# A four-layer graph network on one core: layers 0 and 1 in slots of written order

## The chip, the cores and the metric

The kernel runs on one core of one Trainium2 chip. The metric is device time in microseconds (us): the time of one execution, as a median over runs. A core has five engines that each execute their own stream of instructions: TensorE (PE, matrix products; weight loads are listed apart as PEld), VectorE (DVE), ScalarE (ACT), GpSimd (POOL) and SyncE (SP). They wait for each other through semaphores. Transfers (DMA) are issued by SP, ACT or POOL and run on 16 DMA engines. On-chip memory is SBUF (data) and PSUM (results of PE, in banks of 128 x 512 f32).

## The reference, cut to what matters

`x` is 2708 x 512, `adj` a sparse 2708 x 2708 matrix of non-negative weights whose rows and columns get sparser with their index; all in f32.

```
# layer 0: graph convolution
adj_hat = adj + I;  d = 1/sqrt(rowsum(adj_hat))
x = layernorm(x + (d * adj_hat * d) @ x @ W.T + b)
# layer 1: incidence sum
head = (adj > 0) / max(sqrt(count of positives in the row), EPS)
inc  = adj + head
x = layernorm(x + (inc @ x) / rowsum(inc))
# layer 2: attention over the same neighbours
e  = where(adj != 0, exp(-leaky_relu(s_left + s_right)), 0)
x_a = (e / (rowsum(e) + 1e-5)) @ (x @ W_sa);  x_b = adj @ (x @ W_gcnb) + b_gcnb
x = layernorm(x + sigmoid(attn_a * x_a + attn_b * x_b))   # attn_a, attn_b: gates from adj @ x and x
# layer 3: signs
x = layernorm(x + relu(adj @ (max(sign(x), 0) @ sign(W3).T)))
```

## The kernel before, in words

The 2708 rows are 22 blocks of 128 (the last has 20). Block 0 holds the densest rows and uses all columns. Every other block uses only the columns in which it has a non-zero: up to nine tiles of 128 gathered rows (`ROOM`), many of them for one half of the block's rows only (`HALVES`), plus a few direct tiles (`DIRECT`). Over the blocks these are 107 gathered tiles per layer. Blocks are handled in the order `sequence`: 0, 1, 21, 2, 3, ..., 20.

A first phase (0 to 224 us) loads `adj`, looks for the non-zero columns, gathers the packed weights `packed[b]` and computes `y = x @ W0.T`. It runs inside `in_order()` (L592): instructions traced within it get a dependence on the one before them of the same engine, so that each engine executes them as the program is written. Everything after is ordered by a scheduler, which may put an instruction of a later block before a waiting one of an earlier block on the same engine.

**Layer 0** (224 to 402 us). For each block `b`, POOL gathers rows of `y` by an indirect DMA per tile (`gathered`, L585) into a ring of 10 buffers. PE multiplies each tile with its weights into one PSUM bank (`add_tile`, L1310; two banks of the tag `mm` in turn). DVE adds the bias to the old features (L1401), forms `t` (L1423) and normalises: statistics (L639), aggregate (L641), epsilon (L643), a square root on ACT (L614), a Newton step to the inverse root (L625 to L634), and the scale (L655). SP stores the rows of layer 1's input, `x1_rows`. Between the blocks stand: `count_positive` (L1094, L1096 on DVE, L1098 on PE) and `head_steps` (L1118 to L1150) for layer 1's `head` of each of nine groups of blocks; `attention_columns` (L1335), `attention_rows` and `signs` (L1353, L1354) for later layers; and `grow1` (L1366 to L1370), which adds a finished block's share of block 0's layer 1 sum into the bank `sum1`, two blocks later.

**Layer 1** (402 to 578 us). For each block DVE builds `inc` from the packed weights, up to four tiles at a time (L1564, L1565), POOL gathers rows of `x1_rows` (again L585, 8 buffers), and PE sums (L1310). `finish1` (L1501 on) scales the old features on ACT (L1505), forms `t` on DVE (L1506), normalises with the scale on ACT (L652), multiplies with the row `vr` for the layer 2 score (L1510) and stores `x2_rows` from SP. `grow2` adds one finished block's share of block 0's attention sum, three blocks later: an identity on ACT (L1484), three DVE operations (L1485 to L1487), an exponential (L1488), a copy (L1535), an addition (L1537) and eight products on PE (L1494). ACT holds one set of function tables at a time, so a square root after an exponential reloads them (ACT_TABLE_LOAD), and the other way round. At the start of layer 1 ACT's queue carries the weights of layer 2, the 1 MB `wg` among them.

**Layers 2 and 3** (578 to 1105 us) gather rows of `x2_rows` (L1663) and of `xw_rows`; their code does not change. `open_block` (L1468) opens blocks of layer 2; some of that runs in layer 1.

Of the kernel before, what the change touches and what calls it, by code (L numbers as in the profile page):

```python
# [8 lines left out]
F32 = mybir.dt.float32  # L9
# [5 lines left out]
ALU = mybir.AluOpType  # L15
# [480 lines left out]
def sparse_layers(ctx, tc, x, adj, adj_t, w0_t, b0, w_sa, a_sa, w_gcnb, b_gcnb, wa, ba, wb, bb, w3_t,  # L496
# [140 lines left out]
    def layernorm(dst, t, m: int, name: str, on_pool: bool = False, on_act: bool = False):  # L637
        st = small.tile([P, 6], F32, tag="st", name=f"st_{name}")
        nc.vector.bn_stats(st[:m], t[:m])  # L639
        mv = small.tile([P, 2], F32, tag="mv", name=f"mv_{name}")  # L640
        nc.vector.bn_aggr(mv[:m], st[:m])  # L641
        rs = small.tile([P, 2], F32, tag="rs", name=f"rs_{name}")
        nc.vector.tensor_scalar(mv[:m, 1:2], mv[:m, 1:2], LN_EPS, None, op0=ALU.add)  # L643
        if on_pool:
            nc.gpsimd.tensor_tensor(rs[:m, 0:1], mv[:m, 1:2], neg_half[:m], op=ALU.pow)  # L645
        else:
            rsqrt_of(rs[:m, 0:1], mv[:m, 1:2], m, 1, name)
        if on_act:
            nc.vector.scalar_tensor_tensor(
                rs[:m, 1:2], mv[:m, 0:1], -1.0, rs[:m, 0:1], op0=ALU.mult, op1=ALU.mult  # L650
            )
            return nc.scalar.activation(  # L652
                dst, t[:m], AF.Identity, bias=rs[:m, 1:2], scale=rs[:m, 0:1]
            )
        return nc.vector.tensor_scalar(  # L655
            dst, t[:m], mv[:m, 0:1], rs[:m, 0:1], op0=ALU.subtract, op1=ALU.mult
        )
# [12 lines left out]
    with tc.tile_pool(name="s_pre", bufs=1) as pre:  # L670
# [408 lines left out]
        counts_of = {}  # L1079

        def count_positive(g, pool):

            b0_, G, m = g[0], len(g), rows(g[0])
            hr = ps_s.tile([P, D], F32, tag="find", name=f"hr{b0_}", bufs=2)
            cnt = hr[:, D - GM :]
            counts_of[g] = hr
            at = slice(b0_, b0_ + G)
            nc.vector.tensor_scalar(
                dia_pos[:m, at], dia_own[:m, at], 0.0, None, op0=ALU.is_gt
            )  # L1090
            for k, b in enumerate(g):
                n, nd = tiles(b), len(direct(b))
                valid = small.tile([P, TM], BF16, tag="valid", name=f"valid{b}")
                nc.vector.tensor_scalar(valid[:, : ROOM[b]], index[b], PAD, None, op0=ALU.is_lt)  # L1094
                pos = pool.tile([P, max(ROOM) + 2, P], BF16, tag="pos", name=f"pos{b}", bufs=1)
                nc.vector.tensor_scalar(pos[:, :n, :m], packed[b], 0.0, None, op0=ALU.is_gt)  # L1096
                for i in range(n):
                    nc.tensor.matmul(  # L1098
                        cnt[:m, k : k + 1], pos[:, i, :m],
                        valid[:, i - nd : i - nd + 1] if i >= nd else ones_b,  # L1100
                        start=(i == 0), stop=(i == n - 1),
                    )

        def head_steps(g):
# [8 lines left out]
            def counts():  # L1113
                add_row_sums(g)
                if g == (0,):
                    nc.vector.tensor_tensor(cv, counts0[:, 0:1], counts0[:, 1:2], op=ALU.add)
                else:
                    nc.vector.tensor_tensor(  # L1118
                        cv, counts_of[g][:m, D - GM : D - GM + G], dia_pos[:m, at], op=ALU.add
# [6 lines left out]
            def shares():  # L1126
# [4 lines left out]
                if g == (0,):  # L1131
                    counts_of[g] = ps_s.tile([P, D], F32, tag="find", name="hr0", bufs=2)
                    return
# [5 lines left out]
            def spread():  # L1139
                hr = counts_of[g]  # L1140
# [6 lines left out]
            def keep_heads():  # L1147
                hr = counts_of.pop(g)
# [80 lines left out]


# [86 lines left out]
    with tc.tile_pool(name="s_l0", bufs=10, reuse_waits="tile") as lp:  # L1317
# [22 lines left out]
        def attention_rows():  # L1340
            for s, row in enumerate((vl_row, vr_row)):
                pv = ps_t.tile([P, KC, P], F32, tag="t", name=f"pv{s}")
                for k in range(KC):
                    nc.tensor.transpose(
                        pv[:, k, :], vec[:, s, k : k + 1].to_broadcast([P, P]), ident
                    )
                nc.scalar.copy(row.rearrange("p (k i) -> p k i", i=P), pv)
# [13 lines left out]
        def grow1(j: int):  # L1361
# [14 lines left out]
        between = {  # L1376
            2: [attention_loads], 4: [lambda: attention_columns(0)],
            5: [lambda: attention_columns(1)], 6: [attention_rows],
            8: [lambda: signs(0)], 10: [lambda: signs(1)], 12: [lambda: signs(2)],
            14: [lambda: signs(3)],  # L1380
        }
# [10 lines left out]
        for n, g in enumerate(GROUPS):  # L1392
            steps_ = head_steps(g)
            between.setdefault(2 + 2 * n, []).append(
                several(lambda g=g: count_positive(g, lp), steps_[0])
            )
            between.setdefault(3 + 2 * n, []).append(several(*steps_[1:]))
        for at, b in enumerate(sequence):
            m = rows(b)
            old = place_of_x(b)  # L1400
            nc.vector.tensor_tensor(old[:m, :D], old[:m, :D], b0_row[:m], op=ALU.add)  # L1401
            if b:
# [3 lines left out]
                for i in order_:  # L1406
                    if i >= nd:
                        src[i] = gathered(lp, D, y_rows, b, i - nd)
                    elif direct(b)[i] == b:
                        src[i] = lp.tile([P, D], F32, tag="own", name=f"y_own{b}", bufs=1)  # L1410
# [609 lines left out]
```

## Time and profile before

| | us |
|---|---|
| three runs | 1117.52, 1120.57, 1130.9 (median 1120.57) |
| the profiled execution | 1107.51 |
| its span, first to last instruction | 1105.3 |
| busy in the span: PE, DVE, POOL, ACT | 913.9, 686.0, 522.9, 411.4 |
| layer 0: first gather issued, last gather's end, last store issued | 232.5, 389.1, 401.3 |
| layer 1: the same | 404.2, 559.1, 577.7 |
| layer 2: first and second gather issued | 581.1, 582.4 |
| layer 2: products of block 1's gathered tiles end | 602.2 |

A line of a group names the program's line, the engine, the operation, the tiles it writes and reads and how often it ran; then busy time and the mean of one in ns; then the idle time of that engine just before these instructions and what ended it. A line of waits gives the engine and line that waited, what it waited for, the total in us, how often and the longest. "issue" is time in which nothing shown was waited for. In the chain, each step is followed back from the last instruction to what released it.

### The profile page before, as it was taken

Reading aid. Unit: us, or ns where it says so; the run is one execution under the profiler, and the core shown is the slowest. Engines: PE = TensorE matmul, PEld = TensorE weight load, DVE = VectorE, ACT = ScalarE, POOL = GpSimd, SP = SyncE. Lnnn points to the kernel's source line nnn. Section 1 sums busy time; section 2 is a strip of 40 time slices with the busy share of each in tenths; the row PEclk is TensorE's granted clock in tenths of the full one; section 3 lists DMA queues with packets and bytes.
Section 4 is the critical chain, followed back from the end, with each engine's and each line's share of the span. In section 5 each row is a group of like instructions: output and inputs, shape, how many; then the busy total and the mean of one; then the engine's idle time right before and its main releaser. Section 6 shows DMA issues by size and latency. Waiting matters only on the chain.

```text
span 1105.3 us, 14155 instructions
## 1 busy us (share of the span) xinstructions
PE 913.9 (83%) x4172; PEld 550.5 (50%) x4172; DVE 686.0 (62%) x2812; ACT 411.4 (37%) x918; POOL 522.9 (47%) x539
## 2 busy tenths in 40 slices
PE   3877567768687968888888999999999999889983
PEld 2444334312122312334346577777777777568762
DVE  5766656545565766666774766667667665445665
ACT  3544434300000014556573333333333343254553
POOL 3455555476676637767615143333232232057661
PEclk9888778888889989999999999999999999979996
DMA  9888676276777757767635033332231222289984
GB/s 320 295 275 257 220 241 192 59 218 187 227 212 212 222 164 239 204 204 235 196 116 154 27 110 106 84 104 80 80 106 49 82 79 61 72 257 336 299 248 156
DMA packets 83375, 193.00 MB, mean 175 GB/s; under 512 B 13552, under 2 KB 26712, under 8 KB 83288
## 3 DMA queue, kind: packets, MB, share of 16 engines
q0 software_dynamic: 40048, 111.28, 35.7%
q1 hardware_dynamic: 31548, 65.70, 17.8%
q10 hardware_dynamic: 11692, 15.01, 4.2%
q8 instruction: 35, 0.57, 0.2%
q14 instruction: 52, 0.43, 0.1%
HBM read 156.06 MB, written 25.92 MB: 165 GB/s over the span
## 4 chain that ended last, share of the span: by engine, by line
PE 59%; DVE 11%; issue 8%; another core or an unknown queue 7%; ACT 7%; DMA 6%; POOL 1%; ACTq 0%; SPq 0%; POOLq 0%; DVEq 0%
PE acc L1494 15%; PE l L1310 13%; PE ph L1706 7%; PE l L1889 4%; PE pc L1706 4%; DMA xg<-x_rows,i 4%; PE pg L1706 3%; ACT unused L762 3%; PE l L1928 3%; PE y L1038 2%; PE l L1370 2%; PE px L1756 2%; POOL xg L585 1%; DMA f<-in_x_dram 1%
## 5 line engine op out<-in xcount | busy, mean ns | idle before, releaser
L1663 POOL DMA_INDIRECT xg<-x_rows,i x107 | 105.3, 984 | 158.5 <-PE acc L1494 55.3
L1008 POOL DMA_INDIRECT a<-in_adj_t_dram,row_at x107 | 112.6, 1052 | 116.2 <-DVE s_own L1055 57.2
L585 POOL DMA_INDIRECT xg<-x_rows,i x107 | 106.9, 999 | 63.0 <-issue 24.5
L1494 PE MATMUL acc<-ae,xg 128*128 128x128 f32 (+1 forms) x856 | 125.4, 305 | 6.4 <-ACT ae L1484 2.6
L585 POOL DMA_INDIRECT xg<-y_rows,i x107 | 107.0, 1000 | 49.9 <-issue 24.9
L1494 PEld LDWEIGHTS acc<-ae,xg 128*128 128x128 f32 x856 | 117.0, 191 | 15.8 <-ACT ae L1488 4.1
L1310 PE MATMUL l<-xg,inc 128*64 128x512 f32 (+1 forms) x214 | 91.7, 623 | 17.3 <-DMA xg<-x_rows,i 12.4
L585 POOL DMA_INDIRECT xg<-xw_rows,i x76 | 75.7, 996 | 45.4 <-issue 18.7
L1310 PE MATMUL l<-xg,a 128*64 128x512 f32 (+1 forms) x214 | 92.8, 665 | 2.7 <-issue 1.6
L1038 PE MATMUL y<-s_w,xt 128*128 128x512 f32 (+1 forms) x176 | 93.6, 682 | 0.0
L1706 PE MATMUL ph<-s_wsa,pt 128*128 128x512 f32 (+1 forms) x176 | 79.1, 592 | 0.0
L1494 PE MATMUL acc<-ae,f 128*128 128x256 f32 (+1 forms) x272 | 67.8, 393 | 12.4 <-ACT ae L1535 5.2
L645 POOL TENSOR_TENSOR rs<-mv,s_neg_half 128x1 f32<-128x1 f32 (+1 forms) x22 | 12.6, 571 | 130.4 <-DVE ae L1486 51.4
L1494 PEld LDWEIGHTS acc<-ae,f 128*128 128x128 f32 (+1 forms) x272 | 51.1, 194 | 34.3 <-issue 13.4
L1310 PEld LDWEIGHTS l<-xg,inc 128*64 128x64 f32 (+1 forms) x214 | 24.1, 153 | 74.5 <-issue 43.3
L762 ACT ACTIVATE unused<-arow 128x1408 uint8<-128x1408 f32 (+3 forms) x44 | 58.3, 1325 | 1.5 <-DMA x_rows<-s_zero 0.7
L1484 ACT ACTIVATE ae<-sl,xg 128x64 f32<-128x64 f32 (+1 forms) x107 | 35.9, 362 | 55.7 <-DMA xg<-x_rows,i 28.2
L1038 PEld LDWEIGHTS y<-s_w,xt 128*128 128x128 f32 (+1 forms) x176 | 36.0, 216 | 41.0 <-issue 41.0
L1485 DVE SCALAR_TENSOR_TENSOR ae<-ae 128x128 f32<-128x128 f32 (+4 forms) x95 | 28.2, 297 | 44.2 <-ACT ae L1484 36.1
L1889 PE MATMUL l<-ws,pw 128*128 128x512 f32 (+1 forms) x210 | 52.3, 404 | 2.0 <-DVE pw L1817 2.0
L1928 PE MATMUL l<-xg,p 128*128 128x512 f32 (+1 forms) x152 | 41.6, 418 | 12.2 <-DVE p L1817 11.0
L1706 PE MATMUL pc<-s_wg,pt 128*128 128x258 f32 (+1 forms) x176 | 45.7, 385 | 4.7 <-ACT pt L1693 3.6
(288 smaller groups left out, 1804.8 us busy)
## 6 DMA issues: line engine op xcount, KB each, us to landing
arow<-in_adj_dram SPq DMA_DIRECT2D x21, 704.0 KB
arow<-in_adj_dram SPq DMA_DIRECT2D x21, 650.0 KB
aw<-in_adj_t_dram SPq DMA_DIRECT2D x21, 320.0 KB
x_rows<-f SPq DMA_DIRECT2D x21, 258.0 KB
f<-in_x_dram SPq DMA_DIRECT2D x20, 256.0 KB
y_rows<-yt ACTq DMA_DIRECT2D x20, 256.0 KB
x_rows<-f SPq DMA_DIRECT2D x20, 256.0 KB
out_dram<-f SPq DMA_DIRECT2D x20, 256.0 KB
```

The costliest lines, as they stand in the source:

```text
L585: nc.gpsimd.indirect_dma_start(out=t[:, :dst_w], out_offset=None, in_=src[:, :], in_offset=bass.IndirectOffsetOnAxis(ap=index[b][:, i : i ...
L762: nc.scalar.activation(unused[:m, : ar.shape[1]], ar, AF.Copy, accum_out=row_sums[:m, b, h : h + 1])
L1008: nc.gpsimd.indirect_dma_start(out=packed[b][:, t + len(direct(b)), :], out_offset=None, in_=adj_t, in_offset=bass.IndirectOffsetOnAxis(ap ...
L1038: nc.tensor.matmul(ps[:m], xt[:, k, :m], w0[:, k, :], start=(k == 0), stop=(k == KC - 1))
L1310: nc.tensor.matmul(ps[r0:r1], weights, moving, start=(i == order[0]), stop=all(span(b, j) != (r0, r1) for j in order[order.index(i) + 1 :] ...
L1484: nc.scalar.activation(ev[:, i, :], sl, AF.Identity, bias=score)
L1485: nc.vector.scalar_tensor_tensor(ev, ev, SLOPE, ev, op0=ALU.mult, op1=ALU.max)
L1494: nc.tensor.matmul(acc[:, k, :].rearrange("p (h i) -> p h i", h=2)[:, :, at[0] : at[1]], src[:r, k * P : (k + 1) * P], ae[:r], start=(is_f ...
L1663: nc.gpsimd.indirect_dma_start(out=g, out_offset=None, in_=x2_rows[:, :], in_offset=bass.IndirectOffsetOnAxis(ap=index[b][:, t : t + 1], a ...
L1706: nc.tensor.matmul(ps, pt[:, k, h, :m], w[:, k, :], start=(k == 0), stop=(k == KC - 1))
L1889: nc.tensor.matmul(whole[b], p[:r, h, b * P : (b + 1) * P], g[:r, :], start=(j == 0 and h == 0), stop=(j == NB - 1 and h == 1),)
L1928: nc.tensor.matmul(ps[:m], p[:, h, i * m : (i + 1) * m], src[i0 + i], start=False, stop=(i0 + i == len(src) - 1 and h == 1),)
```

## The change

Layers 0 and 1 are wrapped in `in_order()`, so that each engine executes them as written, and the writing is arranged in slots, one block per slot. A block's sum is started in its slot `at`, and its finish stands two slots later (`LATE = 2`). In layer 0 `grow1` of a block stands four slots after its sum. `layernorm` is split into `layernorm_steps`: between the square root and the Newton step stand the bias addition and `grow1` (layer 0) or `grow2` (layer 1). The sums go through four PSUM banks instead of two, the rings of gather buffers grow from 10 to 13 and from 8 to 11. `count_positive` works one block at a time in slots 1 to 16, the head's spread gets its own PSUM tile, and each `signs(k)` issues its load in its own slot. `inc` is built up to three tiles at a time. In layer 1 `grow2` takes up to three blocks at once; the groups (0,1), (21), (2,3,4), ..., (14,15,16) stand in the loop and (17,18,19) and (20) behind it. The small weight rows of layer 2 are issued from SP instead of ACT, behind the last `x1_rows` store; `wg` and its extra columns move to the start of layer 2, on SP behind the last `x2_rows` store. The sums of `row_sum` are added once, after the first phase.

```diff
+    def layernorm_steps(dst, t, m: int, name: str, on_pool: bool = False, on_act: bool = False):
         st = small.tile([P, 6], F32, tag="st", name=f"st_{name}")
         nc.vector.bn_stats(st[:m], t[:m])
         mv = small.tile([P, 2], F32, tag="mv", name=f"mv_{name}")
         nc.vector.bn_aggr(mv[:m], st[:m])
         rs = small.tile([P, 2], F32, tag="rs", name=f"rs_{name}")
-        nc.vector.tensor_scalar(mv[:m, 1:2], mv[:m, 1:2], LN_EPS, None, op0=ALU.add)
+        v = mv[:m, 1:2]
+        nc.vector.tensor_scalar(v, v, LN_EPS, None, op0=ALU.add)
         if on_pool:
-            nc.gpsimd.tensor_tensor(rs[:m, 0:1], mv[:m, 1:2], neg_half[:m], op=ALU.pow)
+            nc.gpsimd.tensor_tensor(rs[:m, 0:1], v, neg_half[:m], op=ALU.pow)
         else:
-            rsqrt_of(rs[:m, 0:1], mv[:m, 1:2], m, 1, name)
-        if on_act:
-            nc.vector.scalar_tensor_tensor(
-                rs[:m, 1:2], mv[:m, 0:1], -1.0, rs[:m, 0:1], op0=ALU.mult, op1=ALU.mult
-            )
-            return nc.scalar.activation(
-                dst, t[:m], AF.Identity, bias=rs[:m, 1:2], scale=rs[:m, 0:1]
-            )
-        return nc.vector.tensor_scalar(
-            dst, t[:m], mv[:m, 0:1], rs[:m, 0:1], op0=ALU.subtract, op1=ALU.mult
-        )
+            r = small.tile([P, 2, 4], F32, tag="rsqs", name=f"rsqs_{name}")
+            nc.scalar.activation(r[:m, 0, :1], v, AF.Sqrt)
+
+        def rest():
+            if not on_pool:
+                newton(rs[:m, 0:1], v, r[:m, 0, :1], r[:m, 1, :1], 1)
+            if on_act:
+                nc.vector.scalar_tensor_tensor(
+                    rs[:m, 1:2], mv[:m, 0:1], -1.0, rs[:m, 0:1], op0=ALU.mult, op1=ALU.mult
+                )
+                return nc.scalar.activation(
+                    dst, t[:m], AF.Identity, bias=rs[:m, 1:2], scale=rs[:m, 0:1]
+                )
+            return nc.vector.tensor_scalar(
+                dst, t[:m], mv[:m, 0:1], rs[:m, 0:1], op0=ALU.subtract, op1=ALU.mult
+            )
+
+        return rest
...
+        add_row_sums(tuple(range(NB - 1)))
+        add_row_sums((NB - 1,))
...
-    with tc.tile_pool(name="s_l0", bufs=10, reuse_waits="tile") as lp:
+    with tc.tile_pool(name="s_l0", bufs=13, reuse_waits="tile") as lp:
...
+        LATE = 2
+        counted = [(g, k) for g in GROUPS for k in range(len(g))]
+        slot_of = {c: 1 + 16 * n // len(counted) for n, c in enumerate(counted)}
+        for g in GROUPS:
+            last = slot_of[g, len(g) - 1] + LATE
             steps_ = head_steps(g)
-            between.setdefault(2 + 2 * n, []).append(
-                several(lambda g=g: count_positive(g, lp), steps_[0])
-            )
-            between.setdefault(3 + 2 * n, []).append(several(*steps_[1:]))
-        for at, b in enumerate(sequence):
-            m = rows(b)
-            old = place_of_x(b)
-            nc.vector.tensor_tensor(old[:m, :D], old[:m, :D], b0_row[:m], op=ALU.add)
+            put(last + 1, steps_[4])
+            put(last, *steps_[:4])
+        put(20, lambda: attention_spread(0))
+        put(21, lambda: attention_row(0), lambda: attention_spread(1))
+        put(22, lambda: attention_row(1))
+        for c in counted:
+            put(slot_of[c], lambda c=c: count_positive(*c, lp))
+        put(2, attention_loads)
+        put(5, lambda: attention_columns(0))
+        put(7, lambda: attention_columns(1))
+        for k in range(KC):
+            put(9 + 2 * k, lambda k=k: signs(k))
...
-                ps = ps_mm.tile([P, D], F32, tag="mm", name=f"l0_{b}")
+                pool, tag, bufs = SUMS0[at % len(SUMS0)]
+                ps = pool.tile([P, D], F32, tag=tag, name=f"l0_{b}", bufs=bufs)
...
+        def finish0(b: int):
+            m = rows(b)
+            old = place_of_x(b)
             t = work.tile([P, D], F32, tag="t", name=f"t0_{b}")
             nc.vector.scalar_tensor_tensor(
-                t[:m], ps[:m], dinv[:m, b : b + 1], old[:m, :D], op0=ALU.mult, op1=ALU.add
-            )
-            layernorm(old[:m, :D], t, m, f"0_{b}")
-            nc.sync.dma_start(x1_rows[b * P : b * P + m, :], old[:m, :D])
-            for step_ in between.get(at, []):
-                step_()
-        for b in sequence[-2:]:
-            grow1(b)
+                t[:m], sums_of.pop(b)[:m], dinv[:m, b : b + 1], old[:m, :D],
+                op0=ALU.mult, op1=ALU.add,
+            )
+            rest = layernorm_steps(old[:m, :D], t, m, f"0_{b}")
+
+            def store():
+                rest()
+                nc.sync.dma_start(x1_rows[b * P : b * P + m, :], old[:m, :D])
+
+            return store
+
+        SUMS0 = ((ps_mm, "mm", 2), (ps_mm, "sum0", 1), (ps_mm, "mm", 2), (ps_s, "looked", 1))
+        with in_order():
+            for at in range(NB + 2 * LATE):
+                if at < NB:
+                    sum0_of(at, sequence[at])
+                store = None
+                if LATE <= at < NB + LATE:
+                    store = finish0(sequence[at - LATE])
+                if at < NB:
+                    with_bias(sequence[at])
+                if 2 * LATE <= at < NB + LATE:
+                    grow1(sequence[at - 2 * LATE])
+                if store:
+                    store()
+                for step_ in between.get(at, []):
+                    step_()
+                if at >= NB + LATE:
+                    grow1(sequence[at - 2 * LATE])
...
-    wg = wp2.tile([P, KC, D + 2], F32, name="s_wg")
-    nc.scalar.dma_start(wg[:, :, :D], w_gcnb.rearrange("(k p) o -> p k o", p=P))
...
+    with tc.tile_pool(name="s_l1", bufs=11, reuse_waits="tile") as lp:
+        grown2 = []
+
+        def grow2(js):
+
+            r, n, st = rows(js[0]), len(js), state[0]
+            ae = lp.tile([P, G2, 2, P], F32, tag="ae0", name=f"ae0_{js[0]}", bufs=2)
+            av, ev = ae[:r, :n, 0, :], ae[:r, :n, 1, :]
+            a = packed[0][:r, js[0] : js[0] + n, :]
             weights_of(
-                ev[:, None, :], av[:, None, :], st["sl"][:r], a[:, None, :],
-                [f[j][:r, D : D + 1]], f"0_{j}",
+                ev, av, st["sl"][:r], a, [f[j][:r, D : D + 1] for j in js], f"0_{js[0]}"
             )
             nc.scalar.copy(av, a)
-            if n:
-                nc.vector.tensor_tensor(st["esum"][:r], st["esum"][:r], ev, op=ALU.add)
+            if n == 1:
+                nc.vector.tensor_tensor(
+                    st["esum"][:r], st["esum"][:r], ev[:, 0, :], op=ALU.add
+                )
             else:
-                nc.vector.tensor_copy(st["esum"], ev)
-            add_products(0, f[j], ae, r, n == 0, n == NB - 1, (0, P))
-
-        for at, b in enumerate(sequence):
-            m = rows(b)
+                part = st["esum"]
+                if grown2:
+                    part = lp.tile([P, P], F32, tag="part0", name=f"part0_{js[0]}", bufs=1)
+                nc.vector.tensor_reduce(
+                    part[:r, :, None], ev.rearrange("p t i -> p i t"), axis=AX.X, op=ALU.add
+                )
+                if grown2:
+                    nc.vector.tensor_tensor(
+                        st["esum"][:r], st["esum"][:r], part[:r], op=ALU.add
+                    )
+            for i, j in enumerate(js):
+                add_products(
+                    0, f[j], ae[:, i], r, not grown2, len(grown2) == NB - 1, (0, P)
+                )
+                grown2.append(j)
+
+        G2 = 3
+        GROWN2 = [(0, 1), (NB - 1,)] + [
+            tuple(range(j, min(j + G2, NB - 1))) for j in range(2, NB - 1, G2)
+        ]
+        sums_of = {}
+        SUMS1 = (("sum0", 1), ("mm", 2), ("sum1", 1), ("mm", 2))
...
-                for i0, n, (r0, r1) in runs_of(b, 4):
+                for i0, n, (r0, r1) in runs_of(b, 3):
...
+        with in_order():
+            left = list(GROWN2)
+            for at in range(NB + LATE):
+                if at < NB:
+                    sum1_of(at, sequence[at])
+                store = None
+                if at >= LATE:
+                    b = sequence[at - LATE]
+                    store = finish1(b, sums_of.pop(b))
+                if at < NB and left and left[0][-1] in sequence[: max(at - 2 * LATE + 1, 0)]:
+                    grow2(left.pop(0))
+                if store:
+                    store()
+                if at == LATE:
+                    open_block(0, wp2, ps_mm, "mm")
+                    state[0]["acc"] = ps_acc.tile([P, KC, 2 * P], F32, tag="acc", name="acc0")
+            for js in left:
+                grow2(js)
...
+        wg = op.tile([P, KC, D + 2], F32, name="s_wg")
+        nc.sync.dma_start(wg[:, :, :D], w_gcnb.rearrange("(k p) o -> p k o", p=P))
+        pv = ps_s2.tile([P, D], F32, tag="sm", name="pv2")
+        nc.tensor.transpose(pv[:, : 2 * KC], vrows, ident[: 2 * KC, : 2 * KC])
+        nc.vector.tensor_copy(
+            wg[:, :, D:].rearrange("p k t -> p t k"),
+            pv[:, : 2 * KC].rearrange("p (t k) -> p t k", t=2),
```

## The prediction

> **What bounds the kernel now.** I read the page first, then a table of busy time by stage (the stage borders are the first and last instructions of each layer), then the groups and the waits inside layers 0 and 1.
>
> ```profile
> span 1105.3 us, 14155 instructions
> PE 59%; DVE 11%; issue 8%; another core or an unknown queue 7%; ACT 7%; DMA 6%; POOL 1%; ACTq 0%; SPq 0%; POOLq 0%; DVEq 0%
> ```
> ```profile
> 224.00:402.00 178.00, 139.05 (x433) 43.78 (x431) 104.36 (x458) 12.48 (x45) 113.34 (x114) 0.88 0.68 206
> 402.00:578.00 176.00, 143.89 (x408) 59.30 (x407) 116.19 (x508) 94.58 (x164) 106.91 (x107) 0.96 0.67 202
> 640.00:970.00 330.00, 315.35 (x1617) 241.49 (x1615) 210.62 (x792) 118.02 (x337) 94.42 (x104) 0.99 0.29 82
> ```
> Columns after the stretch and its length: busy PE, weight loads, DVE, ACT, POOL, granted clock, DMA share, GB/s. The change works in the first two rows (layers 0 and 1). No engine there is full: 139 to 144 us of PE in 176 to 178. Layer 2 (third row) is PE at 96%, so a delay at its start stays to the end.
>
> ```profile
> L585 POOL DMA_INDIRECT xg<-y_rows,i x107 | 107.0, 1000 | 49.9 <-issue 24.9 <-PE l L1310 11.9 <-remote 6.8
> ```
> ```profile
> L585 POOL DMA_INDIRECT xg<-x_rows,i x107 | 106.9, 999 | 63.0 <-issue 24.5 <-PE l L1310 18.6 <-DMA s_vrows<-in_wb_dram 15.1
> L652 ACT ACTIVATE f<-t,rs 128x512 f32<-128x512 f32 (+1 forms) x22 | 17.6, 810 | 47.0 <-DVE rs L649 16.0 <-DVE rsqs L633 10.6 <-DVE t L1506 10.4
> ```
> ```profile
> DVE inc L1564 <- PE l L1310: 26.0, 16, 6.9
> POOL xg L585 <- PE l L1310: 18.6, 17, 2.8
> ```
> The nearest floor of each layer is POOL's gathers: 107 of them, 1.00 us each and 0.30 us to issue, 1.30 x 107 = 139 us. They now take 157 us (232.5 to 389.1) in layer 0 and 155 (404.2 to 559.1) in layer 1. What stops POOL is a buffer still being read by PE (11.9 and 18.6 us). DVE is only 104 and 116 us busy because a scheduler fills one block's waits with another block's work; even so it waited 26 us before incidence weights for their buffer.
>
> **The change part by part.** *Buffers, banks, LATE.* Three more gather buffers and two more banks take away the wait of POOL for PE: at most 11.9 + 18.6 = 30 us, if POOL stays the limit. Whether it does depends on the order: each engine now executes layers 0 and 1 as the program is written. So I price DVE's written slots by its rows. Between dependent neighbours about 0.05 us passes; independent ones overlap by about 0.07.
>
> *Layer 0, a slot of DVE* (means of rows, us): t 0.747, statistics 0.681, aggregate 0.182, epsilon 0.143, bias 0.682 (fills the square root's trip to ACT), two incidence operations 0.273 + 0.275, Newton 0.154 + 0.210 + 0.141 + 0.151, scale 0.545: 4.2 us, 3.6 without a bias. On top: counts (0.179 + 0.540 less overlap, 0.6) in 16 slots; nine groups of head steps, 14 small operations of 0.15 each with one trip to ACT and one to PE, 2.9 us; two attention columns at 4 x (0.677 + 0.08) = 3.0; four sign steps, 0.428 + 0.680 = 1.2 and about 1.5 until their weights land, because the transfer is issued in the same slot. Slot 3 can start when PE has summed block 1 and counted (249.6 in this trace for the sum, so about 251). Slots 3 to 23 are 21 of them: 17 x 4.2 + 4 x 3.6 = 86, heads 26, counts 8 to 10, columns 6, signs 11: 137 to 140 us, last store of layer 1's input at 389 to 391.5 against 401.3. **Gain 10 to 12 us.** PE needs about 5 us of sums in such a slot. POOL needs 5.1 x 1.30 = 6.6, as much as DVE's mean, but starts 18 us earlier, at 232.5; so both are hidden. If DVE hid too, POOL alone would give a store at 376 to 381.
>
> *Weights' transfers.* The 1 MB of wg leaves the start of layer 1: its first gather took 7.4 us to land, others some 3. Gain 4 us at most, but DVE's order, not the gather, is then next, so I count it only inside the start below. Behind wg's new place on SP (after the last x2 store) nothing of layer 1 queues. The small rows go behind the last x1 store on SP, and one of them waits for PE's last use of the memory it takes; the first x2 store, some 10 us later, is what would wait.
>
> *Layer 1, a slot of DVE.* t 0.741, statistics 0.684, aggregate 0.172, epsilon 0.150, square root on ACT 0.202 and two hand-overs, Newton 0.152 + 0.214 + 0.143 + 0.149, rs 0.149, then the scale on ACT, 0.810, and the product with vr 0.683 + 0.079. Rows 4.33, with ten hand-overs of 0.05: 4.8 us. Now DVE stands idle through the 0.81 us of scale, since the product is next in its order; in the trace of before other blocks' work lay there. Its wait is to be seen even so:
>
> ```profile
> 568.22 0.16 DVE L649 SCALAR_TENSOR_TENSOR rs<-mv,rs 128x1 f32<-128x1 f32 x1
> 568.41 1.52 ACT L652 ACTIVATE f<-t,rs 128x512 f32<-128x512 f32 x2
> ...
> 569.26 0.69 DVE L1510 SCALAR_TENSOR_TENSOR t<-f,s_vr_row 128x512 f32<-128x512 f32 x1 [0.42 <-ACT f L652]
> ```
> 22 finishes x 4.8 = 106. Incidence: 73 pairs x (0.299 + 0.297 less 0.03) = 42. Three openings of layer 2 blocks in it: 12 x (0.679 + 0.077) and small ones, 10. Block 0's sums of threes stand before Newton, so their whole chain is on DVE's order: three ACT scales 3 x 0.392, product 0.6 (the 384-wide incidence operation takes 0.55), 0.33, 0.6, table load 1.283, exp 0.53, reduce 0.6, add 0.2: 5.3 us x 5 groups, 4.1 for the pair, 2.8 for the single: 33. Waiting for block 1's sum at the start: 3. Sum 191 to 194, so with a start at 390 to 392 the last x2 store is at 583 to 586 against 577.7. From the first gather to that store, layer 1 took 173.5 before. **Loss within layer 1 about 18; net of layer 0's gain, 5 to 9 late.** POOL has 22 x 6.6 = 139 to 145 us of work in it and is hidden, and so are its freed waits.
>
> *Table loads.*
>
> ```profile
> L1488 ACT ACT_TABLE_LOAD x16 | 20.5, 1283 | 4.0 <-DVE inc L1564 1.9 <-issue 1.1 <-DVE ae L1487 0.5
> L614 ACT ACT_TABLE_LOAD x16 | 20.5, 1283 | 0.3
> ```
> The groups of three halve 32 loads: 20 us less of ACT. ACT is 95 of 176 us busy, so this shortens nothing by itself. The 7 loads for exp that remain in the loop lie in DVE's chain, 7 x 1.283 = 9 us, already in the 33.
>
> The Trainium skill, ScalarE: Activation LUTs, section What ACT_TABLE_LOAD costs, puts a drain of 1.38 us on top of a load's 1.28. By it the groups would cost 7 x 1.38 = 10 us more and the kernel would end near 1140; the row above shows 0.3 us of idle time before all 16 loads of the square root, so I do not take it.
>
> *Start of layer 2.* After the last x2 store PE has the products of four blocks (groups 17–19 and 20), 4 x 1.99 = 8 us, where two stood before; they need two exp chains of 4 to 5 us after the store. POOL's second gather of layer 2 reuses the memory of the last group, so it waits for its products: about 12 us after the store instead of 4.6 (582.4 against 577.7). wg lands later, so products that filled idle PE between 581 and 585 (2.3 us) come after block 1. End of block 1's first sums: 609 to 611.5 against 602.2. Bounds: 0 if PE's idle time there (588.0 to 598.4 in the chain of waits) swallows it, 5 on top of the store's lateness. I take 3. **Sum: −11 + 18 + 3 = +10.** Layers 2 and 3 are unchanged. By the profiled execution: 1107.5 + 10 = 1117.5 us (span 1105.3 to 1115). That execution is 13.1 us below the median of the three runs shown; I carry the difference over: 1120.6 + 10 = 1130.
>
> **The rivals.** (a) *DVE does not set the slots; POOL does.* DVE was only 104 and 116 us busy, and 41 us of table loads halve. Then both layers go to the gathers' floor: −18 (layer 0) and −16 (layer 1), layer 2's start as before: 1120.6 − 34 = 1087. For it: 17 and 16 us of stalls that buffers and banks address. Against: a sum of DVE's rows with nothing filling the 0.81 us of scale. Somewhere between, with hand-overs at half my price and overlaps elsewhere (layer 0 −15, layer 1 −5, start +2): 1103. (b) *The lockstep also costs layer 0* (slower): PE's counts and head spreads of a slot stand ahead of the next block's sums and wait for DVE's slot to end. It decides once PE's sum (5 us at clock 1, 6 at the 0.88 of the first row) plus counts is longer than the rest of DVE's slot; at 0.6 us in each of 18 slots layer 0 gains nothing, +11 on the forecast, and the layer 1 chain at its upper price (scale and product 1 us more dear in the slots with openings or groups, 10) +6: 1120.6 + 10 + 17 = 1148. (c) *It nets to nothing*: layer 0 −12, layer 1 +12 with DVE overlapping inside groups, start 0: 1120. (d) Gathers back to back raise the DMA share from 0.68 to 0.68 x 157/139 = 0.77; in the pre phase it is 0.98 at 320 GB/s, so this alone I price at 0 to 3 us.
>
> **How the numbers follow.** Forecast 0.36 (1130, own range 1122 to 1140), (b) 0.22 (1140 to 1160), (c) 0.16 (1113 to 1122), between (a) and the forecast 0.12 (1098 to 1113), (a) 0.14 (1080 to 1098). 2%, about what a measurement of this kernel can tell from no change, is 22.4 us: below 1098 faster, above 1143 slower. Faster: (a) 0.14, and some of its neighbour: 0.18. Slower: most of (b): 0.20. Same: 0.62. Leaving out the lower two thirds of (a), 0.10, and the upper half of (b), 0.10, the range is 1092 to 1150.
>
> **What would show it.** Right: DVE over 130 us busy-or-waiting-on-ACT between 250 and the last x1 store near 390; in layer 1 a wait of about 0.8 us of the vr product for the scale, 22 times (17 us); gathers of layer 1 with gaps whose releasers are PE's sums; the last x2 store after 578; POOL's second gather of layer 2 released by PE's acc products. Wrong: gathers spaced 1.30 us all through; a layer 1 of under 170 us; PE idle in layer 0 behind counts; layer 2's first sums at 602 or before.

## The result and the profile after

| | before | changed |
|---|---|---|
| median of four runs, us | 1119.05 | 1174.61 |
| the profiled execution, us | 1107.51 | 1170.99 |
| ratio, 95% interval | | 1.051 (1.041 to 1.061) |

The kernel became 5% slower; the prediction had it 1% slower, and 1174.6 lies above the range. First the changed kernel's page (span, then the chain by engine):

```profile
span 1169.3 us, 14060 instructions
PE 42%; DVE 25%; issue 11%; another core or an unknown queue 7%; ACT 7%; DMA 4%; POOL 2%; ACTq 0%; SPq 0%; POOLq 0%; DVEq 0%
```
DVE's share of the chain went from 11% to 25%, PE's fell from 59% to 42%: in layers 0 and 1 the chain now runs mostly through DVE. The stages, with the same columns as in the prediction (layer 0, layer 1, a stretch of layer 2):

```profile
231.00:419.00 188.00, 125.97 (x429) 42.40 (x428) 129.92 (x469) 10.91 (x44) 112.05 (x114) 0.83 0.65 198
419.00:624.00 205.00, 142.27 (x390) 62.62 (x389) 131.84 (x459) 68.11 (x118) 104.83 (x107) 0.84 0.58 169
690.00:1035.00 345.00, 322.70 (x1650) 248.59 (x1666) 219.12 (x821) 122.78 (x351) 99.55 (x110) 0.99 0.30 82
```
DVE is busy 26 and 16 us more than before, though its instructions' own durations add up to nearly the same: 138 and 145 us in layer 0, 150 and 146 in layer 1. Busy time counts overlapping instructions once, so what went is the overlap of neighbours. PE is busy no more than before; its granted clock fell from 0.88 and 0.96 to 0.83 and 0.84. Groups of POOL, DVE and ACT in layer 1:

```profile
L585 POOL DMA_INDIRECT xg<-x_rows,i x107 | 104.8, 980 | 92.8 <-PE l L1323 36.7 <-issue 26.9 <-DMA s_bab<-in_ba_dram 23.6
```
```profile
L1573 DVE SCALAR_TENSOR_TENSOR t<-f,s_vr_row 128x512 f32<-128x512 f32 (+1 forms) x22 | 15.3, 694 | 20.2 <-ACT f L661 13.8 <-issue 6.3
```
```profile
L661 ACT ACTIVATE f<-t,rs 128x512 f32<-128x512 f32 (+1 forms) x22 | 17.9, 813 | 26.4 <-DVE rs L658 15.7 <-DVE rsqs L625 4.8 <-DVE rsqs L631 2.6
L652 ACT ACT_TABLE_LOAD x8 | 10.3, 1283 | 0.1
L1548 ACT ACT_TABLE_LOAD x7 | 9.0, 1283 | 10.7 <-issue 6.4 <-DVE ae L1547 2.6 <-DVE ae L1546 1.7
```
The table loads did fall from 32 to 15 (8 and 7). POOL waits for PE not less but more: 36.7 us against 18.6, with 11 buffers instead of 8. DVE stands 20.2 us before the product with `vr`, as forecast, and one slot of layer 1 shows how:

```profile
526.81 0.16 DVE L634 TENSOR_TENSOR rs<-rsqs 128x1 f32<-128x1 f32 x1
527.01 0.16 DVE L658 SCALAR_TENSOR_TENSOR rs<-mv,rs 128x1 f32<-128x1 f32 x1
527.25 0.81 ACT L661 ACTIVATE f<-t,rs 128x512 f32<-128x512 f32 x1 [1.11 <-DVE rsqs L625]
...
528.10 0.69 DVE L1573 SCALAR_TENSOR_TENSOR t<-f,s_vr_row 128x512 f32<-128x512 f32 x1 [0.93 <-ACT f L661]
528.71 0.08 DVE L1573 DVE_READ_ACCUMULATOR t<-f,s_vr_row 128x1 f32 x1
528.71 0.29 DVE L1645 SCALAR_TENSOR_TENSOR inc<-a,s_head_row 128x128 f32<-128x128 f32 x1
529.03 0.29 DVE L1646 TENSOR_TENSOR inc<-inc,a 128x128 f32<-128x128 f32 x1
```
Between 527.17 and 528.10 DVE does nothing, though the next block's incidence weights (528.71) wait for nothing: they are written behind the product.

Where the 64 us of span came from, by the issue of stores and gathers: first phase 6.9 (first gather of layer 0 at 239.4 against 232.5); layer 0, first gather to last store, 179.0 against 168.8, 10.2; layer 1, last store to last store, 205.4 against 176.4, 29.0; from there to the end 545.5 against 527.6, 17.9.

### The profile page after: what moved, and what is told of

The parts are those of the page before. It is cut to its first block, busy times and chain, and to the rows that moved or that the text cites. A ratio compares the mean times of both kernels' runs of the same rounds, so it can differ in the third digit from the quotient of the medians.

```text
span 1169.3 us, 14060 instructions
## 1 busy us (share of the span) xinstructions
PE 911.8 (78%) x4153; PEld 563.8 (48%) x4172; DVE 729.5 (62%) x2760; ACT 386.0 (33%) x876; POOL 519.8 (44%) x539
## 4 chain that ended last, share of the span: by engine, by line
PE 42%; DVE 25%; issue 11%; another core or an unknown queue 7%; ACT 7%; DMA 4%; POOL 2%; ACTq 0%; SPq 0%; POOLq 0%; DVEq 0%
PE acc L1554 13%; PE ph L1807 6%; PE l L1990 4%; PE pg L1807 3%; PE pc L1807 3%; PE l L2029 3%; PE y L1049 3%; DVE st L642 3%; POOL xg L585 2%; ACT unused L773 2%; PE px L1857 2%; DMA xg<-x_rows,i 2%; DVE inc L1646 1%; DVE t L1464 1%
## 5 line engine op out<-in xcount | busy, mean ns | idle before, releaser
L1764 POOL DMA_INDIRECT xg<-x_rows,i x107 | 104.4, 976 | 185.6 <-issue 48.8
L585 POOL DMA_INDIRECT xg<-x_rows,i x107 | 104.8, 980 | 92.8 <-PE l L1323 36.7
L1554 PE MATMUL acc<-ae,f 128*128 128x256 f32 (+1 forms) x272 | 75.1, 436 | 34.4 <-ACT ae L1593 19.6
L1323 PE MATMUL l<-xg,inc 128*64 128x512 f32 (+1 forms) x214 | 85.6, 694 | 17.5 <-issue 12.5
L652 ACT ACTIVATE rsqs<-mv 128x1 f32<-128x1 f32 (+1 forms) x44 | 8.9, 203 | 235.6 <-DVE mv L647 127.8
L1554 PEld LDWEIGHTS acc<-ae,f 128*128 128x128 f32 (+1 forms) x272 | 59.5, 222 | 52.1 <-ACT ae L1593 24.1
L1323 PE MATMUL l<-xg,a 128*64 128x512 f32 (+1 forms) x214 | 79.1, 671 | 0.5 <-issue 0.5
L1545 DVE SCALAR_TENSOR_TENSOR ae<-ae 128x128 f32<-128x128 f32 (+5 forms) x82 | 26.3, 321 | 50.8 <-ACT ae L1544 37.8
```

Of the source, the lines that this page charges most:

```text
L585: nc.gpsimd.indirect_dma_start(out=t[:, :dst_w], out_offset=None, in_=src[:, :], in_offset=bass.IndirectOffsetOnAxis(ap=index[b][:, i : i ...
L1323: nc.tensor.matmul(ps[r0:r1], weights, moving, start=(i == order[0]), stop=all(span(b, j) != (r0, r1) for j in order[order.index(i) + 1 :] ...
L1554: nc.tensor.matmul(acc[:, k, :].rearrange("p (h i) -> p h i", h=2)[:, :, at[0] : at[1]], src[:r, k * P : (k + 1) * P], ae[:r], start=(is_f ...
L1764: nc.gpsimd.indirect_dma_start(out=g, out_offset=None, in_=x2_rows[:, :], in_offset=bass.IndirectOffsetOnAxis(ap=index[b][:, t : t + 1], a ...
```

## The experiments

They ran in later sessions on two chips, where the kernel before takes 1005 to 1012 us (granted clock 0.963 instead of 0.924). The changed kernel's ratio there is 1.057, within the result's interval, so ratios are compared, and stages only within these runs. The expectations of the first four give times as in the result's session, where 1% is 11 us. Stages from each profile in us: layer 0 from the first gather to the last `x1_rows` store, layer 1 from there to the last `x2_rows` store, then the rest.

| run | ratio (95%) | layer 0 | layer 1 | rest |
|---|---|---|---|---|
| before_again | 1 | 148.4 | 160.6 | 513.5 |
| after_again | 1.057 (1.053 to 1.062) | 158.5 | 194.7 | 527.0 |
| free_both | 1.0048 (1.0026 to 1.0069) | 152.4 | 161.1 | 517.4 |
| order_l0 | 1.022 (1.017 to 1.027) | 161.6 | 159.4 | 525.4 |
| order_l1 | 1.048 (1.046 to 1.050) | 152.1 | 194.7 | 526.2 |
| few_bufs | 1.058 (1.055 to 1.061) | 165.4 | 195.4 | 522.4 |
| fill_scale | 1.038 (1.033 to 1.043) | 164.7 | 180.0 | 522.2 |
| split_sums | 1.031 (1.028 to 1.034) | 160.1 | 171.1 | 522.5 |
| short_tail | 1.0205 (1.0176 to 1.0234) | 158.2 | 171.7 | 514.3 |
| l0_light | 1.039 (1.036 to 1.042) | 150.1 | 194.4 | 526.6 |
| all_three | 1.0093 (1.0057 to 1.0128) | 150.0 | 172.1 | 518.5 |
| free_three | 0.9976 (0.9957 to 0.9996) | 146.9 | 159.4 | 520.9 |

Five runs share the code of layer 0 (`after_again`, `order_l0`, `fill_scale`, `split_sums`, `short_tail`): 158.2 to 164.7 us, so single profiles scatter by some 6 us in that stage, and smaller differences are not read from it. DVE's wait for the sign weights (`s_neg`, L1371) scatters with it, from 4.2 to 11.4 us. In the rest, the four runs with the changed kernel's layer 1 tail in written order and no other edit there (`after_again`, `order_l1`, `few_bufs`, `l0_light`) lie between 522.4 and 527.0.

The theory: the written order costs, because DVE then stands in its own chain with every wait for ACT in it. The rivals: the larger rings (back to back gathers crowd other transfers), PE or the gathers as the limit, and the start of layer 2.

**free_both, order_l0, order_l1: which layer's order.** The edit, in one or both layers:

```diff
-        with in_order():
+        if True:
```

> The changed kernel with layers 0 and 1 given back to the scheduler (no fixed order); banks, buffers, slots and the grouping of block 0's layer 2 sums stay. Theory A (the fixed order is what costs: DVE stands in its own chain and a wait of one engine holds all others): layer 0 and 1 come back to about 170 and 175 us, the time to 1120 to 1140, what is left being the later start of layer 2. Theory B (the larger rings of buffers cost: back to back gathers fill the DMA engines so that other transfers, instruction loads among them, come late): it stays above 1155. Theory C (the start of layer 2 costs most): stays above 1150 with the last x2 store near 580.

> The changed kernel with only layer 0 in written order, layer 1 free. Theory A: layer 1 comes back to about 176 us from the changed kernel's 206, so about 30 us less, 1140 to 1150. Theory B: no change, above 1165. Theory C: no change in layer 2's start, 527 us from the last x2 store to the end only if the groups at its end run earlier; otherwise 545.

> The changed kernel with only layer 1 in written order, layer 0 free. Theory A: the last x1 store comes at 385 to 400 instead of 418, so 18 to 30 us less, 1145 to 1155. Theory B: no change, above 1165.

Layer 1's order alone costs 1.048 - 1.005, so 4.3%, layer 0's alone 1.7%; together 6.0% where the whole change costs 5.2% over `free_both`. All the rest of the change (banks, rings, slots, groups of three, moved weights) is worth +0.5%. Rival B falls by `free_both`: it has the larger rings and is within 0.5% of the kernel before. In two points the forecast was off. `order_l1` was to gain 18 to 30 us, 1.6 to 2.7%, over the changed kernel and gained 0.9%; its layer 0 fell by 6.4 us, and taken alone it fits rival B's "no change". And `order_l0` keeps 525 us for the rest although layer 1 is free, so the rest is not layer 1's order alone (its second gather comes 13.7 us after the store, that of `free_both` 5.8).

**few_bufs: the rings.**

```diff
-    with tc.tile_pool(name="s_l0", bufs=13, reuse_waits="tile") as lp:
+    with tc.tile_pool(name="s_l0", bufs=10, reuse_waits="tile") as lp:
...
-    with tc.tile_pool(name="s_l1", bufs=11, reuse_waits="tile") as lp:
+    with tc.tile_pool(name="s_l1", bufs=8, reuse_waits="tile") as lp:
```

> The changed kernel with rings of 10 and 8 gather buffers as before, all else as changed. Theory A: DVE sets the pace, so 0 to 5 us either way, 1168 to 1180. Theory B: the waits at the start of both layers (instructions that come late while the DMA engines are full: about 12 and 7 us) go, 1150 to 1160.

1.058 against the changed kernel's 1.057: under the written order three more buffers bring nothing that the times show. In `before_again` they have little to bring; its group of layer 0's gathers:

```profile
L585 POOL DMA_INDIRECT xg<-y_rows,i x107 | 105.9, 990 | 32.6 <-issue 13.1 <-DMA xg<-y_rows,i 8.8 <-PE l L1310 8.5
```
105.9 busy and 32.6 idle, most of it the 0.30 us after each gather, is 138.5 us: the gathers of the kernel before are at the floor of 139 us that the prediction computed. In its layer 1 they take 140.7 us from the first gather to the last one's end.

> The kernel before, for a profile on the same chip as the next three. Both theories: ratio 1.00; layer 1 about 160 to 176 us between the last stores of the layers, layer 2 on 517 to 527 us from the last x2 store to the end.

> The changed kernel, for a profile and a ratio on the same chip as the next two. Theory A (DVE's written order): ratio 1.045 to 1.06, layer 1 some 195 us between the last stores of the layers.

**fill_scale: the wait for the scale.** The edit, inside the loop over slots of layer 1 (`rest` ends with the scale on ACT, `store` is the product and the store):

```diff
                 if at < NB:
                     sum1_of(at, sequence[at])
-                store = None
+                if store:
+                    store()
+                rest = store = None
                 if at >= LATE:
                     b = sequence[at - LATE]
-                    store = finish1(b, sums_of.pop(b))
+                    rest, store = finish1(b, sums_of.pop(b))
...
-                if store:
-                    store()
+                if rest:
+                    rest()
```

> The changed kernel with one move in layer 1: a block's product with the vr row and its store stand behind the next slot's incidence weights, so that DVE has work while ACT scales. Theory A1 (DVE's chain sets layer 1, its price is the sum of its rows with their waits): the 20 us of waiting for the scale go and layer 1 is 15 to 20 us shorter. Rival (PE at its lowered clock, or the gathers, set layer 1): less than 5 us shorter, and DVE waits for PE's sums instead.

Layer 1 fell by 14.7 us, at the lower edge of the forecast, the ratio from 1.057 to 1.038. DVE's waits in layer 1, first of `after_again`, then of `fill_scale`:

```profile
DVE t L1573 <- ACT f L661: 20.1, 22, 1.0
DVE part L1602 <- ACT ae L1548: 9.6, 5, 1.9
DVE ae L1545 <- ACT ae L1544: 8.7, 7, 2.0
DVE sl L1536 <- PE slp L1534: 8.1, 1, 8.1
```
```profile
DVE part L1601 <- ACT ae L1548: 9.6, 5, 1.9
DVE ae L1545 <- ACT ae L1544: 9.5, 8, 2.0
DVE sl L1536 <- PE slp L1534: 8.4, 1, 8.4
...
DVE t L1572 <- ACT f L661: 2.7, 3, 0.9
```
17.4 us of the first wait go, no other of these rows grows by more than 0.8 us, no wait for PE's sums comes in their place.

**split_sums: the exponential and the opening.** A group of three is cut in three: `grow2` does the part up to the exponential, `middle` the exponential and the copy on ACT, `late`, a slot later, the reduction, the addition and the products. `if late:` stands behind the next slot's product:

```diff
-                    grow2(left.pop(0))
+                    middle, late = grow2(left.pop(0))
                 if rest:
                     rest()
+                if middle:
+                    middle()
...
                 if store:
                     store()
+                if late:
+                    late()
```

> As fill_scale, and block 0's sums of threes cut in two: exponentials issued on ACT after the scale, their reduction and products a slot later; and the copy of the opened block 0's row a slot later. Theory A1: DVE loses its waits for the table load and the exponential too (about 12 us) and the one for the opening (8), layer 1 another 12 to 20 us shorter than fill_scale. Rival: another 0 to 5 us, and waits for PE take their place.

Another 8.9 us of layer 1, less than forecast. The reduction's waits went (9.6 to 1.7), the one for the opening did too, but DVE now waits 10.0 us for PE's sums to free incidence tiles: a part of the rival came true.

**short_tail: the start of layer 2.**

```diff
-            tuple(range(j, min(j + G2, NB - 1))) for j in range(2, NB - 1, G2)
-        ]
+            tuple(range(j, j + G2)) for j in range(2, 17, G2)
+        ] + [(17, 18), (19,), (20,)]
...
-                if at < NB and left and left[0][-1] in sequence[: max(at - 2 * LATE + 1, 0)]:
+                if left and left[0][-1] in sequence[: max(at - LATE, 0)]:
```

> As split_sums, with block 0's last groups cut to (17,18), (19), (20) and started a slot earlier, so that after the last x2 store only the products of one or two blocks are left instead of four. Theory D (the tail of the sums holds POOL's second gather and cools PE's clock; it costs the 9 to 13 us by which layer 2 on is longer than before): the last x2 store to the end falls from 522 to 527 us to 514 to 518, ratio about 1.02 to 1.025. Rival (the late transfer of wg costs it): no change within 2 us.

The rest falls from 522.5 to 514.3, before's 513.5 within 1. `wg` comes as late as in the changed kernel (issued 0.4 us after the store in both), so that rival falls. PE and POOL after the last `x2_rows` store, first in `after_again` (store at 533.0), then in `short_tail` (508.3); only the lines that matter:

```profile
537.09 9.51 PE L1554 MATMUL acc<-ae,f 128*128 128x256 f32 x32 [8.96 <-ACT ae L1593]
537.11 0.95 POOL L1764 DMA_INDIRECT xg<-x_rows,i  x1 [31.07 <-issue]
...
547.36 0.94 POOL L1764 DMA_INDIRECT xg<-x_rows,i  x1 [9.30 <-DVE ae L1546]
...
549.30 6.78 PE L1554 MATMUL acc<-ae,f 128*128 128x256 f32 x16 [2.22 <-ACT ae L1548]
```
```profile
509.40 3.72 PE L1558 MATMUL acc<-ae,f 128*128 128x256 f32 x16 [0.49 <-ACT ae L1600]
512.51 0.94 POOL L1792 DMA_INDIRECT xg<-x_rows,i  x1 [32.85 <-DVE sl L1537]
...
513.87 0.94 POOL L1792 DMA_INDIRECT xg<-x_rows,i  x1 [0.42 <-issue]
...
516.32 3.69 PE L1558 MATMUL acc<-ae,f 128*128 128x256 f32 x16 [2.73 <-DVE ae L1771]
```
In `after_again` PE stood still 8.96 us, took 9.51 us for 32 products that need 7.4 to 8 at full clock (16 in 3.69, 8 in 1.99), and 6.78 for the next 16, which take 3.69 in `short_tail`; the second gather came 14.4 us after the store, in `short_tail` 5.6. What the gathers cost and what PE's products cost is not separated: in `few_bufs`, with the changed kernel's tail, the second gather comes 5.2 us after the store (the third 12.3), and the rest still takes 522.4.

**l0_light: DVE in layer 0.**

```diff
-            rest = layernorm_steps(old[:m, :D], t, m, f"0_{b}")
+            rest = layernorm_steps(old[:m, :D], t, m, f"0_{b}", on_act=True)
...
+            put(7 + 2 * k, lambda k=k: signs_load(k))
             put(9 + 2 * k, lambda k=k: signs(k))
```

> The changed kernel with layer 0's scale moved from DVE to ACT (which is idle there) and the four loads for the signs issued two slots ahead. Theory A2 (DVE's written chain sets layer 0): its rows fall by 22 x (0.55 - 0.16) = 9 us and the waits for the loads by 4 to 12, so layer 0, first gather to last x1 store, falls from 158 to 165 us to 145 to 150; ratio 1.04 to 1.045. Rival (PE, or the gathers with their floor of 134 to 139 us, set layer 0): less than 4 us shorter, DVE waits for PE instead.

Layer 0 fell to 150.1 us, 8 below the least of the five with the same layer 0 and 1.7 above before's 148.4; `all_three` repeats it (150.0). Neither PE's nor POOL's work was touched, so DVE's written chain set layer 0 as well. The gathers do not differ: their last one ends at 318.6 us in `before_again`, 318.8 in `after_again` and 317.0 in `l0_light`; the last store follows 10.2, 19.5 and 11.5 us later. The two edits were not tried apart. Against `after_again` DVE's busy time fell by 8.9 us and its wait for the sign weights by 4.5, while its waits for the square roots of the `head` steps grew by 4.5.

**all_three and free_three.** Both take the edits of `short_tail` and `l0_light`; `free_three` has no written order in layers 0 and 1.

> short_tail and l0_light together, both layers still in written order. If the terms are separate, they add: layer 0 about 148, layer 1 about 170, layer 2 on 516 us: ratio 1.01 to 1.02. If POOL or PE takes over as the limit, less than the sum of both.

> all_three with both layers given back to the scheduler. Theory A: the written order was the cost, and the smaller DVE chain and tail leave it at 0.99 to 1.005. Rival (the scheduler gains nothing from a lighter DVE because POOL's gathers already run at their floor): equal to free_both within 0.5%.

The terms of layers 0 and 1 add (150.0 and 172.1). The rest is 4 us longer than in `short_tail`, and the two traces show where: in both PE stands before the same 16 products, 2.74 and 2.73 us, but in `all_three` its granted clock has just fallen to 0.50, and the products take 6.51 us against 3.69; 32 later ones take 5.47 against 3.84. That is 4.4 us. In layer 1 the written order still costs 13 us (172.1 against `free_three`'s 159.4); where these lie was not tried. `free_three` is the only version at or below the kernel before, by 0.24%, an interval that barely leaves out 1.

## Why the prediction was wrong, point by point

The span of the profiled execution grew by 64 us where 10 were forecast: layer 0 by 10.2 (forecast -11), layer 1 by 29.0 (18), the start of layer 2 and what follows by 17.9 (3), the first phase by 6.9 (0). The step that failed most is the comparison: the new chain, added up from clean rows, was held against stage times of the kernel before that a slower session had lengthened.

- **"Sum 191 to 194" for layer 1: right within 1 us in the experiments, 11 to 14 too low in the result.** In the experiments it measures 194.7, and the waits priced in it are there (20.1 us for the scale against 0.81 x 22 = 18; 11.4 for the reductions of the groups). One that it left out is there too: 8.1 us for PE before the copy of the opened block 0's row (`sl`). With it the sum would be 199 to 202, so other terms were 4 to 7 us too dear, and that much of the agreement is luck. In the result's profile the stage took 205.4; this one wait is 15.7 there, and the remainder is not explained.
- **"Loss within layer 1 about 18": wrong, +34 (experiments) and +29 (result).** The sum was held against before's 173.5, a measured stage in which the engines had stood for other reasons. In the experiments the kernel before took 160.6 for the same work. A sum of clean rows was set against a disturbed time. Moreover 173.5 runs from the first gather to the last store, while the sum runs from store to store, where before took 176.4.
- **"Gain 10 to 12 us" in layer 0: wrong in sign, +10 in the result's session and in the experiments.** The chain from block 1's `t` to the last store, put at 137 to 140, measures 142 in `after_again` (196.2 to 338.3); `before_again` needs 133 (195.9 to 328.8). In the result's profiles the two are 149 (269.1 to 418.4) and 146 (255.0 to 401.3). The prediction took the 401.3 with its delays and let its own chain begin at 251 and run without any. That there were delays can be seen in the profile of before, in DVE's waits:

```profile
DVE pos L1096 <- remote: 21.9, 4, 9.7
```
and there are such waits in the changed kernel too, one of 7.29 us before the same instruction (L1096 is L1106 there):

```profile
261.00 0.17 DVE L1104 TENSOR_SCALAR valid<-i 128x7 bf16<-128x7 int32 x1
268.45 0.69 DVE L1106 TENSOR_SCALAR pos<-a 128x1024 bf16<-128x1024 f32 x1 [7.29 <-remote]
269.06 0.74 DVE L1464 SCALAR_TENSOR_TENSOR t<-l,s_dinv,f 128x512 f32<-128x512 f32 x1
```

How much of the lost time these waits are is not shown: the longest of before, 9.73 us in front of this instruction, is 12.29 in `before_again`, put down to PE there. What is shown is that from the first gather to block 1's `t` the result's two profiles need 22.5 and 29.7 us, `before_again` and `after_again` 15.6 and 16.4.

- **"I take 3" for the start of layer 2: +13.5 and +17.9.** The held second gather was forecast (12 us after the store; 14.4 measured), but the price was bounded as if PE's idle time could swallow it and as if PE ran at full clock. Its clock was 0.56 on the mean of the first 10 us after the store. `short_tail` comes within 1 us of before, `all_three` with the same tail within 5.
- **Buffers and banks ("at most 30 us, if POOL stays the limit").** The condition failed, as the prediction feared: `few_bufs` changes nothing in the time.
- **The rivals.** (a) fell: POOL set neither layer of the changed kernel, and in the experiments the gathers of the kernel before already run at their floor. "Gathers spaced 1.30 us all through" was named as a sign against the forecast; in layer 0 of `after_again` they are (106.7 us busy, 32.6 idle), and DVE still sets the last store. (b) had the side right and the mechanism wrong: layer 0's order costs 1.7% (`order_l0` against `free_both`, about half of it in the rest), but moving work off DVE gives layer 0's part back, and from block 1's `t` on DVE waits for PE only 4.7 us in `after_again`, so it was DVE and not PE behind the counts. (d) shows nowhere.
- **What stays open.** Why the result's session lengthened the stages. The first phase is 6.9 us longer in the result's profile; in the experiments it is not (first gather at 179.8 against 180.4). What "remote" stands for was not tried: these waits are in the result's two profiles and in none of the experiments'. The Trainium skill, Runtime: NRT & Kernel Launch, section Instruction fetch mechanics, says that code arrives in blocks by DMA and that a taken branch breaks the prefetch; that could be it, but no run here shows it.

In sums: 10.1 + 34.1 + 13.5 - 0.6 (first phase) = 57.1 us in the experiments, the difference of the spans 1060.0 and 1002.9.

## What to carry to other kernels

A written order takes away the cover that a scheduler finds: add up the new chain with every wait in it, and hold it against the old stage's own undisturbed work (its busy rows and its floor), not against its measured time, which holds delays that the new kernel will have as well. If an order is to be written, put nothing behind a wait that doesn't need it: moving one product behind the next block's weights gave 15 us. And look at what is left for the end of a stage: four blocks' sums after the last store held the next stage's gathers and left PE standing until its clock fell.

## What the runs showed of the hardware

- Read in steps of 0.2 us around the last `x2_rows` store, PE's granted clock is 0.50 or 1.00 (but for the steps in which it changes), and within one run its changes lie multiples of 3.41 us apart: in `after_again` down at 531.6, up at 541.9, down at 548.7, up at 555.5 us; in `all_three` down at 493.4, up at 496.8, down at 507.1, up at 513.9, down at 524.1, up at 527.6; in `short_tail` down at 500.9, up at 507.7. Its means of 0.56, 0.78 and 0.87 in the first three stretches of 10 us after the store of `after_again` are mixtures of the two. The length of PE's standing does not decide alone: after 2.74 us the clock was down in `all_three`, after 2.73 us it was up in `short_tail`. The Trainium skill, TensorE: Matmul & The Clock Gate, section What's actually happening, says that the gate closes to half after an idle window of about 3.4 us. The fall at 531.6, 3.5 us after PE's last product, agrees; the fall at 507.1 came 1.6 us after the last one, so here the measurement differs. In layer 1 as a whole the clock was 0.94 in `before_again` and 0.89 in `after_again`.
- An exponential started 1.29 us after its table load did. The Trainium skill, ScalarE: Activation LUTs, section What ACT_TABLE_LOAD costs, adds a drain of 1.38 us to every switch of tables; it is not to be seen here, and leaving it out of the sum was right. In `before` a load starts at 480.87, the square root at 482.16, the next load at 482.38 and the exponential at 483.68, with no room for a drain on either side of a load. From `after_again`:

```profile
469.38 1.28 ACT L1548 ACT_TABLE_LOAD   x1 [1.73 <-DVE ae L1547]
...
470.67 0.52 ACT L1548 ACTIVATE ae<-ae 128x384 f32<-128x384 f32 x1
```
- The same kernel took 1119 us in one session and 1005 in another, with the first phase, layer 0 and layer 1 of before 52, 20 and 16 us shorter; the ratio of the two kernels hardly moved (1.051 and 1.057).
